# A Perceiver layer on one core: order of the opening, of late loads, and of norm steps

## The chip, the cores and the metric

The kernel runs on one core of a Trainium2 chip. The core has a matrix engine (TensorE, "PE" in the profile, with its weight loads as "PEld"), three engines for elementwise work (VectorE "DVE", ScalarE "ACT", GpSimd "POOL") and an engine that here only issues transfers (SyncE, "SP", its queue "SPq"). Each engine takes its instructions in order and waits on semaphores for the others. The metric is the device time of one execution in microseconds; less is better.

## The reference

Three sub-layers are applied to x, 16 batches of 64 rows of 512 (1024 rows in all), each with a residual: a cross-attention in which the layer-normed x supplies the latents, a differential self-attention over the 64 rows of a batch, and a gated feed-forward whose inputs and weights are rounded to blockwise FP4.

```
x = x + xattn(ctx, layernorm(x))
    ln = LN(latents) * g_l + b_l;  xn = LN(ctx) * g_x + b_x
    q = ln @ w_q;   k, v = split([xn ; ln] @ w_kv)
    out = LN(softmax(q k^T / 8, over 512 context rows and the 64 latents) v @ w_out) * g_o + b_o
x = x + attn(layernorm(x))
    rope on q and k; o = softmax(q1 k1) v - lam * softmax(q2 k2) v; rms norm; @ Wo^T
x = x + ffn(layernorm(x))
    h = silu(fp4(x) @ fp4(w_gate)^T) * (fp4(x) @ fp4(w_up)^T);  fp4(h) @ fp4(w_down)^T
```

All inputs are float32.

## The kernel before

The 1024 rows of x are eight tiles of 128 rows (`cm.x[0]` to `cm.x[7]`), two batches to a tile. The precision of float32 is kept by splitting both factors of a product into a high half, rounded to the matrix engine's float32r, and a low half, the remainder. A product is then three terms, high x high, high x low and low x high, each over four slices of 128 of the inner dimension: `Common.terms` (L114) issues one term per step of a generator, `Common.product` runs all three. Making the halves is a cast (mostly ScalarE) and a subtraction (VectorE or GpSimd).

The program has four stages:

- `_latents` (L455) normalises the tiles of x, turns each on PE (`turn`), scales and shifts it while it is copied out of PSUM (`ln`, L518 and L520), makes its halves (`halves`, L523) and multiplies by w_k, w_q and w_v, two tiles (a "group") at a time. `heads` (L589) makes k or q of a group: four products `lk_g_m` or `lq_g_m` of 128 x 256, each copied to `kst` or `qst` by `take`; `values` makes v. The results go to DRAM. For the first group's k, the variable `late` makes the products of m = 0, 1 and 2 issue their first two terms one product after the other, and the third terms only afterwards, since the low halves of w_k come last. Side work (the weights of w_v, the scaled weights for the context, the bias sums, the statistics of later tiles, the first context batches) is put on a list with `during(n, ...)`; `then()`, called once after each product, runs what the list has for that number.
- `cross_attention` (L723) takes one batch b after another: keys and values of the 512 context rows (`pk`, `pv`), scores (`sim`), a masked softmax, the weighting (`av`). `begin(b)` loads the mask, the queries and the latents' values of a batch, `around(b, m)` loads the latents' keys into the two ends of a key tile. `cx.load(b)` loads the whole context of a batch (`nat`, 1 MB) for its statistics, `cx.fetch` the transposed context in four pieces. `load_o` and `weight_o` load and split w_out during batch 0. Once the first batch is under way, `quant.tick()` runs a step of the FP4 rounding of the feed-forward weights.
- `SelfAttention.rest` (L1362) runs the tiles of the self-attention as a pipeline; the first two are worked in at the end of the cross-attention. In iteration n it makes q, k and v of tile n, adds the output of tile n-2 to x (`out`, the addition at L1339), and `end(n)` makes the transposes, the scores and the softmax. Between these it runs steps of the feed-forward's norm of tiles 0 and 1: `norm_steps` gives seven for a tile, namely moments, shift and scale, and five of the FP4 rounding. `parts[n]` says how many steps stand at each of two places of iteration n: after `rope(n, "Wk")` and after `out(n - 2)`.
- `FeedForward.rest` runs gate, up and down products for the eight tiles.

What sets the order: up to the end of `SelfAttention.rest` the instructions of an engine run in the order in which the program lists them (`Common.in_order`, called at its end, ties each one to the one before it on its engine). Only the rest of the feed-forward is placed by the scheduler of the framework, which may put its instructions among earlier ones. SP's transfers, too, are issued in program order, and a transfer whose buffer is still in use, or whose completion semaphore is still taken by an earlier one, holds up all transfers behind it.

PSUM has three buffers for products and transposes (`cm.mm`, `cm.tr`), two double ones for scores (`cm.two`), and one more. Weights on their way to be split have nine buffers (`raw`): eight are taken by w_k and w_q and the ninth by the first quarter of w_v; the other three quarters of w_v wait until halves of w_k are done.

The opening's order before, as `_latents` lists it: load x tile 0, the four vectors of the norm (`cw.load`), x tile 1, w_k, w_q, the first of w_v, x tiles 2 and 3; moments of both tiles; norm of both; turn of both; halves (high, then low) of tile 0; the casts of w_k; halves of tile 1; the low halves of w_k, those of k = 1 and 3 on GpSimd; then w_q likewise.

Of the kernel before, what the change touches and what calls it, by code (L numbers as in the profile page):

```python
# [14 lines left out]
ALU = mybir.AluOpType  # L15
# [4 lines left out]
P = 128  # L20
# [25 lines left out]
def f32(t):  # L46

    return t.bitcast(F32)
# [406 lines left out]
def _latents(ctx, tc, cm, sc, i, cw, cx, sa):  # L455
# [22 lines left out]
    def high(name, w, k):  # L478
        nc.scalar.copy(w[0][:, k, :], raws[name, k])

    def low(name, w, k):
        by = (nc.vector, nc.gpsimd)[k % 2]
        by.tensor_tensor(w[1][:, k, :], raws[name, k], f32(w[0][:, k, :]), ALU.subtract)

    def split(name, w, *ks):
# [34 lines left out]
                nc.scalar.activation(ln[:, k, :], src, AF.Identity, bias=bias, scale=scale)  # L520
        rows[p] = ln

    def halves(p):  # L523
        g, n = divmod(p, GT)
        ln = rows.pop(p)
        hi, lo = (t[:, :, n * P : (n + 1) * P] for t in lns[g])
        nc.vector.tensor_copy(hi, ln)
        nc.vector.tensor_tensor(lo, ln, f32(hi), ALU.subtract)

    def bias(name, k):  # L530

# [45 lines left out]
    def during(n, do, *args):  # L577

        todo.setdefault(n, []).append((do, args))
# [9 lines left out]
    def heads(g, what, w, dst, scale, bias=None):  # L589

        hi, lo = lns[g]
        st = pool.tile([P, KC, GT * P], F32, tag=f"{what}st", name=f"{what}st_{g}")

        def take(m, ps):
            if bias is None:
                nc.scalar.copy(st[:, m, :], ps)
            else:
                nc.scalar.activation(
                    st[:, m, :], ps, AF.Identity, bias=bias[:, m : m + 1], scale=scale
                )  # L600


        late = 3 if (g, what) == (0, "k") else 0
        made = []
        for m in range(KC):
            cols = slice(m * P, (m + 1) * P)
            ps = cm.mm(f"l{what}_{g}_{m}")[:, : GT * P]
            terms = cm.terms(
                ps,
                lambda k, cols=cols: (w[0][:, k, cols], w[1][:, k, cols], hi[:, k, :], lo[:, k, :]),  # L610
                range(KC),
            )
            made.append((m, ps, terms))
            if m < late:
                next(terms)
                next(terms)
            if m < late - 1:
                continue
            for at, done, steps in made:
                for _ in steps:  # L620
                    pass
                then()
                take(at, done)
            made = []
        nc.sync.dma_start(dst[g], st)

    def values(g):
# [11 lines left out]
            nc.scalar.copy(vst, ps)  # L639
            nc.sync.dma_start(sc.v[p], vst)  # L640

    load(0)
    cw.load(pool)
    load(1)
    weight("k", *range(KC))
    weight("q", *range(KC))
    weight("v", 0)
    load(2, 3)
    moments(0)
    moments(1)  # L650
    cw.turn()
    norm(0)
    norm(1)
    high("k", w_k, 0)
    turn(0)
    turn(1)
    halves(0)
    for k in range(1, KC):
        high("k", w_k, k)
    halves(1)  # L660
    for k in range(KC):
        low("k", w_k, k)
    for k in range(KC):
        high("q", w_q, k)
    for k in range(KC):
# [4 lines left out]
    cx.load(0)  # L670
    for k in range(KC):
        during(0, bias, "q", k)
    during(3, bias_sum, "q", cw.bq, S**-0.5)
    during(16, sa.turn_norm)
    for k in range(KC):
        during(1 + k, high, "v", w_v, k)
# [31 lines left out]
    during(19, cx.load, 1)  # L708
    during(22, cx.every, 0)
    during(39, cx.spread, 1)  # L710
    during(39, cx.load, 2)
    for g, _ in enumerate(groups):
        heads(g, "k", w_k, sc.k, 1.0)
        heads(g, "q", w_q, sc.q, S**-0.5, cw.bq)
        if g + 1 < len(groups):
            for p in groups[g + 1]:
                turn(p)
                halves(p)
        values(g)
    assert not todo  # L720

# [1 line left out]
def cross_attention(tc, cm, sc, i, cw, cx, w1, w2, att, quant):  # L723
# [259 lines left out]
    mask(0)  # L983
    around(0, 0, 1, 2, 3)
    around(1, 0, 1)
    for b in range(B):

        def tick():
            if b:
                quant.tick()  # L990

        done = (b - 3) // 2 if b >= 3 and b % 2 else None
        last = b == B - 1
        keys(b, 0)
        if last:
            att.load("Wq")
            att.load("Wk")
        cx.high(b + 1, 0)
        if b >= 4 and b % 2 == 0:
            out_moments((b - 4) // 2)  # L1000
        tick()
        keys(b, 1)
        cx.low(b + 1, 0)
        cx.high(b + 1, 1)
        tick()
        if b:
            turn_both(b - 1)
            turn_latents(b - 1)
        if done is not None:
            out_turn(done)  # L1010
        keys(b, 2)
        cx.fetch(b + 2, 0)
        cx.flat(b + 1)
        cx.low(b + 1, 1)
        cx.high(b + 1, 2)
        tick()
        if last:
            att.split("Wq", 0, 1)
        if b:
            finish(b - 1)  # L1020
        tick()
        if last:
            att.split("Wq", 2)
        scores(b, 0)
        softmax(b, 0)
        around(b + 1, 2, 3)
        keys(b, 3)
        cx.fetch(b + 2, 1)
        cx.low(b + 1, 2)
        cx.high(b + 1, 3)  # L1030
        tick()
        values(b, 0)
        cx.every(b + 1)
        cx.low(b + 1, 3)
        cx.stats(b + 2, 0)
        tick()
        if last:
            att.split("Wq", 3)
            att.load("Wv")
        if b == 0:  # L1040
            load_o(0)
            load_o(1)
        values(b, 1)
        begin(b + 1)
        cx.fetch(b + 2, 2)
        cx.stats(b + 2, 1)
        tick()
        if b == 0:
            weight_o(0)
            weight_o(1)  # L1050
            load_o(2)
            load_o(3)
        if last:
            att.norm(0)
            att.split("Wk", 0, 1)
        turn(b, 0, 0)
        turn(b, 0, 1)
        scores(b, 1)
        softmax(b, 1)
        around(b + 2, 0, 1)  # L1060
        if done is not None:
            out_product(done)
        quant.tick()
        values(b, 2)
        cx.fetch(b + 2, 3)
        cx.stats(b + 2, 2)
        quant.tick()
        if done is not None:
            out_norm(done)
            out_add(done)  # L1070
        if b == 0:
            weight_o(2)
            weight_o(3)
        if b == 2:
            att.sa.load()
        if b == 5:
            att.sa.work()
        if last:
            att.split("Wk", 2, 3)
            att.load("Wo")  # L1080
            att.turn(0)
        values(b, 3)
        cx.stats(b + 2, 3)
        cx.spread(b + 2)
        mask(b + 1)
        quant.tick()
        cx.load(b + 3)
    turn_both(B - 1)
    turn_latents(B - 1)
    att.product(0, "Wq")  # L1090
    att.split("Wv", 0, 1)
    finish(B - 1)
    att.rope(0, "Wq")
    att.split("Wv", 2, 3)
    att.norm(1)
    att.product(0, "Wk")
    att.rope(0, "Wk")
# [14 lines left out]
    att.norm(2)  # L1112
    out_product(NT - 1)
    att.split("Wo", 2, 3)
    att.end(1)
    out_norm(NT - 1)
    assert not quant.active and not quant.jobs
    return {2: lambda: out_add(NT - 1), 3: lambda: out_moments(NT - 1)}

# [1 line left out]
class SelfAttention:  # L1121
# [240 lines left out]
    def rest(self, ff, last):  # L1362
# [2 lines left out]


        first, second = (ff.norm_steps(t) for t in range(2))
        norms = iter(first[:5] + second[:1] + first[5:] + second[1:])


        parts = {3: (1, 1), 4: (1, 1), 5: (2, 2), 6: (2, 1), 7: (1, 2)}

        def steps(n, part):
            for _ in range(parts[n][part] if n in parts else 0):
# [2 lines left out]
        for n in range(2, NT):  # L1377
# [21 lines left out]
                ff.weights(("g", 0), ("u", 0))  # L1399
            steps(n, 1)  # L1400
            self.end(n)
        assert not list(norms)
        ff.gate((0, 0))
        self.scale(NT - 2)
# [292 lines left out]
```

## Time and profile before

The median of three runs is 925.25 us (924.92 to 925.33). The profile is of one execution, which took 924.27 us; its span, from the first to the last instruction, is 922.5 us. One line of a timeline has the start in us, the busy time in us, engine, line of the code, operation, output and inputs by their names, shapes and count; in brackets stands how long the engine had been idle and what ended it.

| stretch, us | what runs | PE idle in it, us |
|---|---|---|
| 0 to 20 | loads, first norms, first k products | 12.6 |
| 20 to 92 | the rest of the latents' stage | 0.0 |
| 92 to 135 | batch 0 and the start of batch 1 of the cross-attention | 3.0 |
| 135 to 574 | batches 1 to 15 | 0.0 |
| 574 to 725 | self-attention | 5.0 |
| 725 to 922.5 | feed-forward | 4.5 |

The matmuls of the first products (128 x 256) follow each other every 0.213 us until 19.0 us and every 0.12 us from then on. In the middle of the kernel a product of 128 x 512 (12 matmuls) takes PE 2.7 us, one of 128 x 256 1.44 us.

### The profile page before, as it was taken

The page shows a single profiled execution, that of the slowest core. Times are in us where ns is not written, and L with a number is a line of the kernel's source. Part 1 is how long each engine was busy: PE and PEld are TensorE (multiplying, and loading weights), DVE is VectorE, ACT ScalarE, POOL GpSimd, SP SyncE. Part 2 cuts the span into 40 slices and gives each one's busy share as a digit, 9 for nine tenths or more (in the row PEclk, how much of TensorE's full clock was granted, in tenths as well). Part 3 has the DMA queues.
Part 4 walks back from the last instruction along what each step waited for, and adds up shares of the span by engine and source line. Part 5 has one row for each costly group of instructions (what it writes and reads, how often), then busy time and mean ns, then how long its engine had stood idle before and what let it go on. Part 6 is the DMA issues. An engine that isn't in the chain of part 4 may idle for free.

```text
span 922.5 us, 17526 instructions
## 1 busy us (share of the span) xinstructions
PE 897.4 (97%) x6774; PEld 741.2 (80%) x6774; DVE 683.2 (74%) x1384; ACT 392.3 (43%) x750; POOL 328.4 (36%) x378
## 2 busy tenths in 40 slices
PE   4999999999999999999999999999999999999998
PEld 4998778778877887887878877777888788888886
DVE  6545457878799787786987864575888698888875
ACT  4465255544545444444444445444344333323221
POOL 3245143326344363263443622556474321100000
PEclk9999999999999999999999999999999999999999
DMA  6464556454555455345544351140005630000000
GB/s 232 180 222 145 161 149 189 137 182 145 162 142 162 152 163 170 111 141 146 168 137 150 122 177 70 47 183 1 2 1 201 234 137 12 12 12 12 12 12 23
DMA packets 80234, 111.11 MB, mean 120 GB/s; under 512 B 33160, under 2 KB 38808, under 8 KB 78872
## 3 DMA queue, kind: packets, MB, share of 16 engines
q1 hardware_dynamic: 79992, 109.48, 36.9%
q8 instruction: 53, 0.87, 0.4%
q0 software_dynamic: 160, 0.52, 0.2%
q14 instruction: 29, 0.24, 0.1%
HBM read 84.26 MB, written 25.72 MB: 119 GB/s over the span
## 4 chain that ended last, share of the span: by engine, by line
PE 84%; DVE 7%; ACT 3%; POOL 2%; DMA 2%; SPq 1%; issue 1%; ACTq 0%; DVEq 0%; POOLq 0%
PE pv L121 18%; PE pk L121 18%; PE gu L121 13%; PE dn L121 7%; PE av L898 4%; PE sim L830 4%; PE prt L171 3%; PE lk L121 3%; PE lq L121 3%; PE lv L121 2%; PE po L121 2%; PE wo L121 2%; DVE ex L1239 1%; PE Wv L121 1%; PE ht L171 1%
## 5 line engine op out<-in xcount | busy, mean ns | idle before, releaser
L121 PE MATMUL pv<-xvh,x 128*128 128x512 f32 x512 | 133.4, 392 | 1.1 <-ACT prT L865 1.1
L121 PE MATMUL pk<-x,xkh 128*128 128x512 f32 x512 | 130.4, 397 | 0.0
L121 PEld LDWEIGHTS pv<-xvh,x 128*128 128x128 f32 x512 | 95.2, 188 | 24.7 <-issue 2.6
L121 PEld LDWEIGHTS pk<-x,xkh 128*128 128x128 f32 x512 | 93.7, 188 | 25.4 <-issue 3.9
L817 ACT ACTIVATE v<-pv,rs 128x512 f32<-128x512 f32 x64 | 43.9, 686 | 78.8 <-PE pv L121 78.7
L804 DVE TENSOR_TENSOR k<-pk,row 128x512 f32<-128x512 f32 x64 | 43.7, 684 | 45.1 <-PE pk L121 45.1
L368 POOL TENSOR_TENSOR x<-raw,x 128x512 fp32r<-128x512 f32 x32 | 44.2, 1383 | 79.4 <-ACT x L362 79.4
L853 ACT ACTIVATE pr<-pr,least 128x576 f32<-128x576 f32 x64 | 49.2, 772 | 52.4 <-DVE least L849 52.1
L121 PE MATMUL pk<-x,xkl 128*128 128x512 f32 x256 | 68.6, 390 | 0.0
L121 PE MATMUL pv<-xvl,x 128*128 128x512 f32 x256 | 68.5, 389 | 0.0
L121 PE MATMUL gu<-uT,fx 128*128 128x512 f32 (+1 forms) x288 | 67.2, 377 | 0.0
L121 PE MATMUL gu<-gT,fx 128*128 128x512 f32 (+1 forms) x288 | 65.5, 375 | 1.1 <-DVE h L1533 0.6
L121 PEld LDWEIGHTS gu<-gT,fx 128*128 128x128 f32 x288 | 52.3, 188 | 9.0 <-ACT fx L129 0.9
L121 PEld LDWEIGHTS gu<-uT,fx 128*128 128x128 f32 x288 | 51.9, 188 | 7.3
L121 PEld LDWEIGHTS pk<-x,xkl 128*128 128x128 f32 x256 | 48.1, 188 | 10.3
L121 PEld LDWEIGHTS pv<-xvl,x 128*128 128x128 f32 x256 | 48.1, 188 | 10.2
L849 DVE CUSTOM_DVE_ANT_0 pr<-sim,mask 128x576 f32<-128x576 f32 x64 | 45.9, 755 | 9.9 <-PE sim L830 9.1
L121 PE MATMUL dn<-dT,hh 128*128 128x512 f32 x176 | 44.8, 394 | 0.6 <-ACT hh L129 0.6
L205 ACT ACTIVATE qe_h<-qe_h,mmagic 128x512 f32<-128x512 f32 (+1 forms) x24 | 16.5, 688 | 67.2 <-DVE qe_h L202 64.0
L321 DVE BATCH_NORM_STATS2 cst<-nat 128x6 f32<-128x512 f32 x64 | 42.8, 669 | 0.0
L865 ACT COPY prT<-prt 128x512 f32<-128x512 f32 x64 | 34.1, 585 | 18.0 <-PE prt L171 18.0
L898 PEld LDWEIGHTS av<-v,prT 128*64 128x64 f32 x1024 | 36.7, 138 | 5.6 <-issue 5.6
(303 smaller groups left out, 1972.7 us busy)
## 6 DMA issues: line engine op xcount, KB each, us to landing
nat<-in_ctx_dram SPq DMA_DIRECT2D x16, 1024.0 KB
raw<-in_ctxT_dram SPq DMA_DIRECT2D x64, 256.0 KB
d_d<-qhl_d SPq DMA_DIRECT2D x11, 512.0 KB
row<-rs_d SPq DMA_DIRECT2D x16, 256.0 KB
g_d<-qhl_g SPq DMA_DIRECT2D x8, 512.0 KB
u_d<-qhl_u SPq DMA_DIRECT2D x8, 512.0 KB
gT<-g_d SPq DMA_DIRECT2D x4, 1024.0 KB
uT<-u_d SPq DMA_DIRECT2D x4, 1024.0 KB
```

The source lines that it names most:

```text
L121: self.nc.tensor.matmul(ps, lhsT=p[i], rhs=p[j], start=start and n == 0, stop=stop and n == last)
L171: self.nc.tensor.transpose(pt[:, c * P : (c + 1) * P], src[:, c * P : (c + 1) * P], self.ident)
L205: nc.scalar.activation(e, e, AF.Relu, bias=self.mmagic, scale=MAGIC)
L321: nc.vector.bn_stats(st, self.nat[b][:, j, :])
L368: by.tensor_tensor(lo, self.raw[:, c, :], f32(hi), ALU.subtract)
L804: nc.vector.tensor_tensor(k[:, S : S + N], ps, cx.row[b], ALU.mult)
L817: nc.scalar.mul(v, ps, cx.rs[b][:, t : t + 1])
L830: nc.tensor.matmul(pss[r][c * S : (c + 1) * S, h, :half], lhsT=queries[b % 2][rows, m, :], rhs=st["k"][m][rows, at : at + half], start=Tru ...
L849: nc.vector.tensor_tensor_reduce(two(pr), ps[:, :, :half], two(mask), -1.0, BIG, ALU.add, ALU.min, least)
L853: nc.scalar.activation(pr, pr, AF.Exp, bias=least, scale=-1.0, accum_out=st["tot"][:, t : t + 1])
L865: nc.scalar.copy(prT, pt.rearrange("p (j q) -> p j q", q=P))
L898: nc.tensor.matmul(st["av"][rows, 2 * a + r, :], lhsT=w[:, rows], rhs=v[:, at : at + S], start=(n == 0), stop=(n == len(pairs) - 1),)
```

## The change

- The loads of x tiles 0 and 1 are issued first, ahead of the norm's vectors. norm(0) stands ahead of moments(1) on VectorE.
- `halves` is cut in two: `upper` makes the high half of a tile, `lower` the low one. Both tiles' high halves come first, then both low ones. All four low halves of the first w_k are made by VectorE; the others keep their alternation between VectorE and GpSimd.
- In `heads`, the products that are made together (three for the first k, one elsewhere) issue their first terms, then their second, then their third. Their calls of `then()` all come next, and only then the copies. For the first q the copies lag two products behind (`lag`), and the bias sum of q moves from list number 3 (with k's last product) to 5 (with q's second).
- `cx.load(2)` moves from the end of the latents' stage behind the first `around` loads of the cross-attention.
- w_out: `weight_o(0)`, `weight_o(1)` and the loads of quarters 2 and 3 move, within batch 0, from after `values(0, 1)` to after `values(0, 2)`; `weight_o(2)` and `weight_o(3)` move to batch 1, after `keys(1, 1)`.
- At the end of the cross-attention, quarters 2 and 3 of Wv are split ahead of `finish(B - 1)`, and `out_norm(NT - 1)` stands ahead of `att.end(1)`.
- The norm steps have a third place, after `end(n)`; the order of the two tiles' steps and their shares change. First-tile steps are f0 to f6 and second-tile steps s0 to s6: before, n = 3: f0 | f1; 4: f2 | f3; 5: f4 s0 | f5 f6; 6: s1 s2 | s3; 7: s4 | s5 s6. After, n = 3: f0 | - | f1; 4: f2 s0 | f3 | s1; 5: f4 | f5 | f6; 6: s2 | s3 | -; 7: s4 | s5 | s6.

```diff
-    def low(name, w, k):
-        by = (nc.vector, nc.gpsimd)[k % 2]
+    def low(name, w, k, by=None):
+        by = by or (nc.vector, nc.gpsimd)[k % 2]
...
-    def halves(p):
-        g, n = divmod(p, GT)
-        ln = rows.pop(p)
-        hi, lo = (t[:, :, n * P : (n + 1) * P] for t in lns[g])
-        nc.vector.tensor_copy(hi, ln)
-        nc.vector.tensor_tensor(lo, ln, f32(hi), ALU.subtract)
+    def upper(*tiles):
+        for p in tiles:
+            g, n = divmod(p, GT)
+            nc.vector.tensor_copy(lns[g][0][:, :, n * P : (n + 1) * P], rows[p])
+
+    def lower(*tiles):
+        for p in tiles:
+            g, n = divmod(p, GT)
+            hi, lo = (t[:, :, n * P : (n + 1) * P] for t in lns[g])
+            nc.vector.tensor_tensor(lo, rows.pop(p), f32(hi), ALU.subtract)
...
         late = 3 if (g, what) == (0, "k") else 0
-        made = []
+        lag = 2 if (g, what) == (0, "q") else 0
+        made, ready = [], []
...
             made.append((m, ps, terms))
-            if m < late:
-                next(terms)
-                next(terms)
             if m < late - 1:
                 continue
-            for at, done, steps in made:
-                for _ in steps:
-                    pass
+            for _ in range(3):
+                for _, _, steps in made:
+                    next(steps)
+            for _ in made:
                 then()
-                take(at, done)
+            ready += made
             made = []
+            while len(ready) > lag:
+                take(*ready.pop(0)[:2])
+        for at, done, _ in ready:
+            take(at, done)
...
-    load(0)
+    load(0, 1)
     cw.load(pool)
-    load(1)
...
     moments(0)
-    moments(1)
     cw.turn()
     norm(0)
+    moments(1)
     norm(1)
     high("k", w_k, 0)
     turn(0)
     turn(1)
-    halves(0)
     for k in range(1, KC):
         high("k", w_k, k)
-    halves(1)
+    upper(0, 1)
+    lower(0, 1)
     for k in range(KC):
-        low("k", w_k, k)
+        low("k", w_k, k, nc.vector)
...
-    during(3, bias_sum, "q", cw.bq, S**-0.5)
+    during(5, bias_sum, "q", cw.bq, S**-0.5)
...
-    during(39, cx.load, 2)
...
                 turn(p)
-                halves(p)
+                upper(p)
+                lower(p)
...
     around(1, 0, 1)
+    cx.load(2)
...
         keys(b, 1)
+        if b == 1:
+            weight_o(2)
+            weight_o(3)
...
-        if b == 0:
-            weight_o(0)
-            weight_o(1)
-            load_o(2)
-            load_o(3)
...
         if b == 0:
-            weight_o(2)
-            weight_o(3)
+            weight_o(0)
+            weight_o(1)
+            load_o(2)
+            load_o(3)
...
     att.split("Wv", 0, 1)
+    att.split("Wv", 2, 3)
     finish(B - 1)
     att.rope(0, "Wq")
-    att.split("Wv", 2, 3)
...
     att.split("Wo", 2, 3)
+    out_norm(NT - 1)
     att.end(1)
-    out_norm(NT - 1)
...
-        norms = iter(first[:5] + second[:1] + first[5:] + second[1:])
-        parts = {3: (1, 1), 4: (1, 1), 5: (2, 2), 6: (2, 1), 7: (1, 2)}
+        norms = iter(first[:3] + second[:1] + first[3:4] + second[1:2] + first[4:] + second[2:])
+        parts = {3: (1, 0, 1), 4: (2, 1, 1), 5: (1, 1, 1), 6: (1, 1, 0), 7: (1, 1, 1)}
...
             self.end(n)
+            steps(n, 2)
```

## The prediction

> **What bounds the kernel.** The page's first part shows PE busy 97% of 922.5 us, so only places where PE waits can pay. The table of stretches (length, PE busy with its instructions, clock, DMA share, GB/s) says where these are:
>
> ```profile
> 0.00:20.00 20.00, 7.39 (x33) 1.00 0.66 223
> 20.00:92.00 72.00, 72.00 (x505) 1.00 0.52 186
> 92.00:135.00 43.00, 40.05 (x279) 1.00 0.57 166
> 135.00:574.00 439.00, 439.00 (x3336) 1.00 0.49 149
> 574.00:725.00 151.00, 145.98 (x1654) 1.00 0.24 93
> ```
>
> Between 20 and 92 us and between 135 and 574 us PE never rests: a PE instruction that comes earlier there brings the end forward one for one. The losses are 12.6 us in the opening, 3.0 where the cross-attention starts, 5.0 in the self-attention; the change touches all three. The waits of PE, and the timeline around them:
>
> ```profile
> PE lk L121 <- DVE lnh L527: 5.7, 1, 5.7
> PE pv L121 <- ACT prT L865: 1.1, 1, 1.1
> PE av L898 <- ACT prl L883: 1.0, 1, 1.0
> PE sim L830 <- DMA mask<-q_d: 0.9, 1, 0.9
> ```
> ```profile
> 9.94 2.67 POOL L483 TENSOR_TENSOR wkl<-raw_k,wkh 128x512 fp32r<-128x512 f32 x2 [2.51 <-ACT wkh L479]
> 10.41 1.08 DVE L527 CAST lnh<-ln 128x512 fp32r<-128x512 f32 x1
> 11.52 1.64 DVE L528 TENSOR_TENSOR lnl<-ln,lnh 128x512 fp32r<-128x512 f32 x1
> ...
> 13.08 1.48 DVE L527 CAST lnh<-ln 128x512 fp32r<-128x512 f32 x1
> 14.60 1.64 DVE L528 TENSOR_TENSOR lnl<-ln,lnh 128x512 fp32r<-128x512 f32 x1
> ...
> 14.71 1.20 PE L121 MATMUL lk<-lnh,wkh 128*128 128x256 f32 x4 [5.70 <-DVE lnh L527]
> ```
>
> The first product waits for the second tile's first half, which ends at 14.56, behind the first tile's second half. Each of these four VectorE steps takes over twice its undisturbed time (0.43 and 0.69 us at 31.81 and 32.27), while GpSimd makes weight halves.
>
> **Opening (loads, halves, staged terms).** SP issues x tile 1 at about 1.18 instead of 2.57; the four vector rows move back 0.4 us and land at about 4.5, wanted by ScalarE's ln at 7. On VectorE norm(0) now comes before moments(1): GpSimd's mv is ready at 5.24, so norm(0) runs at 5.3 (was 6.06), moments(1) at 5.8, its GpSimd pair until 7.7, norm(1) 7.7 to 8.25 (was 7.84: 0.4 later). PE turns tile 1 by 9.4, VectorE's four ln steps (1.37) end at 10.9. Then both casts: 0.43 each, GpSimd idle, since its k halves are gone and its q halves wait for raw_q 1, which ScalarE casts until 12.28. So hi is complete at 11.8 and PE starts at 11.85, 2.85 earlier. The twelve first terms need only that; at the cold pitch of 0.213 they last until 14.4.
>
> Here a rule must be weighed. By the rows, a VectorE step beside GpSimd is slower by 1.64/0.69 = 2.4; so counted, the second lo ends at 14.0, the k halves at 15.3, 15.9, 16.5 and 17.1. The Trainium skill (SBUF — State Buffer, "Who interferes with whom") says instead that a VectorE instruction with two SBUF inputs, or in a two-port mode, and a GpSimd one lock each other out for a whole instruction. That fits the ends better: GpSimd's four subtractions (9.94 to 15.69) and VectorE's four halves end in strict turn, at 11.20, 11.49, 12.61, 13.16, 14.28, 14.56, 15.69, 16.24. I take it. GpSimd keeps q halves 1 and 3: the first holds up lo 1 (ends 14.05), the second k half 0 (ends 15.75); the others follow at 16.4, 17.0, 17.6. Second terms: 14.4 to about 16.8. Third terms of m=0 wait for k half 3: done 17.8; m=1 and m=2 (0.48 each) 18.8.
>
> Product m=3 needs the PSUM buffer of m=0, hence its copy on ScalarE, and all three `then()` now precede it: it queues behind the casts of v 0 and v 1. raw_v 1 takes the buffer of a weight half; the first one went at 11.20 (GpSimd's half 1), now at 15.75. SP issues it at 15.8, it lands about 2.7 later (its row: 11.23 to 13.75 and on), cast until 19.2, copy until 19.6. So m=3 starts at 19.65, ends at 21.1. The bias sum (0.9) moves from before q to after q's second product, so q ends at 21.1 + 4x1.44 + 0.9 = 27.8, against 29.57. **Gain 1.8** (by the factor 2.4 it would be 2.35). If that raw load is late there is less: 0.8; with no wait for it 2.6. The q copies, two products late, wait for bq at about 25.0, before q's last product wants the buffer. norm(3) then ends at about 27.4, just in time: VectorE is next in line.
>
> A second rule speaks against hoping for more: the Trainium skill (TensorE: Matmul & The Clock Gate, Part 1) has the first 3.4 us or so of activity at half clock whatever is issued, by a free-running window. The row: cold pitch 0.213 from 14.71 to 19.02 (4.3 us), then 0.117. By the row the second terms end at 16.8, by the rule at 15.9, with a missed window at 17.0; each time k half 3 (17.6) and the copy (19.6) decide. Nothing is added for it.
>
> **Cross-attention start.** nat_2 (1 MB, SP at 90.62) now goes after the `around` loads.
>
> ```profile
> 93.85 0.64 SPq L762 DMA_DIRECT2D mask<-q_d  x1
> ...
> 98.84 0.45 SPq L792 DMA_DIRECT2D k<-k_d  x1
> 99.59 0.44 SPq L793 DMA_DIRECT2D k<-k_d  x1
> ...
> 100.80 2.23 PE L830 MATMUL sim<-k,mask 64*64 64x288 f32 x16 [0.88 <-DMA mask<-q_d]
> 101.50 0.19 PEld L830 LDWEIGHTS sim<-k,mask 64*64 64x64 f32 x2 [0.51 <-DMA k<-k_d]
> 101.85 0.67 PEld L830 LDWEIGHTS sim<-k,mask 64*64 64x64 f32 x10 [0.16 <-DMA k<-k_d]
> ```
>
> The 128 KB of queries took 6.8 us to land beside it, and SP's k issue at 98.84 waited 1.36 on nat's completion semaphore. Without it that pair goes at 97.5 and 98.15, lands 2.25 later (as 99.59 to 101.85) at 100.4, and PE resumes there instead of at 101.85: **gain 1.45** (0.7 to 2.0). nat_2 is then issued at about 104.4 (in the old run's times). Its first reader stands on VectorE at 107.56 and may wait to about 110; next in that queue is the softmax minimum at 113.5, with statistics of 1.8 between: room, cost 0.
>
> weight_o(0, 1) leaves ScalarE's queue ahead of prT: there the casts at 115.55 waited 3.35 for raw_wo, and PE lost 1.24 at 117.45. Now prT copies run at about 112, **gain 1.2**. SP also loses the two load_o that held the k loads and the first qw_g behind them, so VectorE no longer waits for qw_g (8 us idle before 124.53). The bill comes in batch 1: weight_o(2, 3), 1.24 of ScalarE and 2.6 of GpSimd, now stand ahead of prT and prl for which PE lost 1.17 at 131.26; VectorE's exponent mask (1.52 beside GpSimd at 127.69) is still ahead of them too. Ends: all 1.17 gone, or 0.6 more. I take **0.5 gained**.
>
> **Self-attention.** Wv's halves 2 and 3 before finish(15): GpSimd's last one moves from 590.50 to 584.9, PE's 0.5 at 591.85 goes: **0.5**; VectorE and GpSimd are idle there, and rc_k follows in time. out_norm before end(1): oz (0.81 at 617.33) moves to about 609.4, into an idle of 2.45 on VectorE; the `on` that PE awaits starts 0.7 earlier, still after GpSimd's rstd at 617.1: **0.7** of the 0.93 at 618.79. Norm steps: at n=3 the ScalarE step fz (642.75, waiting 2.86 for mv_f) moves behind end(3), so qT comes 1.0 earlier and PE's wait at 644.09 goes: **1.0**. But at n=4 begin of tile 1 joins slot 0, ahead of the x addition that frees wt's buffer:
>
> ```profile
> 657.60 1.22 DVE L196 TENSOR_SCALAR qm_x<-qs_x 128x32 f32<-128x32 f32 x1
> 658.85 0.35 DVE L197 RECIPROCAL qm_x<-qm_x 128x32 f32<-128x32 f32 x1
> 659.12 0.63 DVE L1339 TENSOR_TENSOR x<-wo,x 128x512 f32<-128x512 f32 x1
> ```
>
> The addition is already late by 0.3; bn_stats and bn_aggr (0.69 + 0.18 + a gap) add **1.0 lost** (0.7 to 1.3). At n=6 the step fz leaves but qm's four remain behind GpSimd's adds: 0. n=5 and n=7 have cover (the addition ran as soon as wo ended): 0.
>
> **Sum.** 1.8 + 1.45 + 1.2 + 0.5 + 0.5 + 0.7 + 1.0 - 1.0 = 6.15. The profiled execution took 924.27 (span 922.5 and 1.8 around it) and becomes 918.1; the median, 925.25, is 1.0 above it and becomes **919.1**.
>
> **Rivals.** (a) As worked out, each term within its ends: 917.5 to 920.5, 0.60. (b) The opening hardly pays: raw_v 1, or norm(3), holds PE until 29; the opening gives 0.3, total 4.6, 920.6; for it: all raw loads are bandwidth-bound here (223 GB/s), against: SP issues nothing else at 15.8. 0.14. (c) ScalarE's wo casts move PE's loss to batch 1 (131.26 grows by 0.6) and the k loads still land late: total about 4.0, 921.3. 0.12. (d) The n=4 loss doesn't come, since the scheduler's order leaves VectorE free earlier: 917.5 or below, 0.09. (e) Slower: nat_2 lands late. VectorE stands in order at its statistics, and behind it the softmax minimum of batch 0's second half; PE wants what follows (pr turned at 126) 11 us after it. Landing 8 us after issue (as at 90.62) costs nothing; from 17 us on each us is lost, and 24 us would pass 925.25: 926 or more. No transfer of the trace is near that. 0.03. That the parts cancel or the change does nothing: 0.02.
>
> 0.2% (1.85 us) is what a measurement can tell from no change. Faster 0.94, same 0.03, slower 0.03. Range: 916.8 to 921.8, which takes in (b) and (c).
>
> **What would show it.** First lk matmul at about 11.9 and lq's last before 28; no wait at the former 117.45 and 591.85; sim's wait under 0.7; wt at n=4 waiting about 1.5 for x. Wrong if m=3 of lk waits past 20.5, if the av wait doubles, or if VectorE is seen standing at nat_2's statistics beyond 5 us.

## The result, and the profile after

The changed kernel takes 918.08 us (median of four runs, 917.56 to 919.49) against 925.29 for the kernel before in four runs beside it: ratio 0.9925, 95% interval 0.9911 to 0.9939. The profiled execution took 917.56 us, its span is 915.8, so 6.71 of execution and 6.7 of span are gone. Line numbers below are those of the changed kernel, up to 8 off for the same line.

The table of stretches of the kernel after (length, PE busy with its instructions, granted clock, DMA share, GB/s):

```profile
0.00:20.00 20.00, 10.78 (x61) 1.00 0.76 252
20.00:90.00 70.00, 69.17 (x479) 1.00 0.53 183
90.00:130.00 40.00, 39.40 (x283) 1.00 0.59 178
...
570.00:720.00 150.00, 145.56 (x1653) 1.00 0.25 98
```

The opening's loss fell from 12.6 to 9.2 us, that at the cross-attention's start from 3.0 to 0.6, that of the self-attention from 5.0 to 4.4. New is 0.8 us of loss in the stretch from 20 on, which had none before. The waits of PE (line waited for: total, times, longest; the first of the list, for the norm's vectors, is left out) name it:

```profile
PE lt L171 <- DVE lz L155: 3.0, 4, 1.2
PE lk L121 <- DVE lnh L526: 2.3, 1, 2.3
PE wt L1282 <- DVE x L1346: 1.4, 2, 1.1
PE ot L171 <- DVE on L1318: 0.8, 1, 0.8
...
PE av L904 <- ACT prl L889: 0.6, 1, 0.6
```

The wait of lk went from 5.7 to 2.3; those of `pv` for prT and of `sim` for the queries are off the list. Two waits grew: `lt`, the turn of a tile that norm(3) feeds, and `wt`, as forecast.

Where the gain arose is read by lining up the same matmul in both traces. This ledger is worked out from their start times; a negative lead means that the kernel after is ahead.

| at the matmul of (time before) | lead, us | step | forecast |
|---|---|---|---|
| lv, first (30.36) | -2.08 | -2.08 | -1.8 |
| sim of batch 0, last (102.63) | -4.07 | -1.99 | -1.45 |
| pv after prT (117.45) | -5.31 | -1.24 | -1.2 |
| av after prl (131.26) | -5.85 | -0.54 | -0.5 |
| Wv (591.85) | -6.38 | -0.53 | -0.5 |
| ot after `on` (618.79) | -7.31 | -0.93 | -0.7 |
| zt at n = 3 (644.09) | -8.25 | -0.94 | -1.0 |
| wt at n = 4 (659.80) | -7.52 | +0.73 | +1.0 |
| ot at n = 6 (685.71) | -6.81 | +0.71 | 0 |
| end | -6.69 | +0.12 | |

Every term came with its sign and within about half a us, but for the last +0.71, which was not foreseen. The step at `av` is the least certain: the experiments show how far it varies.

The opening's inside went otherwise than worked out. The timeline of the kernel after, VectorE and GpSimd from 10 us on (start, busy):

```profile
10.81 0.76 DVE L526 CAST lnh<-ln 128x512 fp32r<-128x512 f32 x2
11.48 1.29 DVE L532 TENSOR_TENSOR lnl<-ln,lnh 128x512 fp32r<-128x512 f32 x2
12.68 2.50 DVE L483 TENSOR_TENSOR wkl<-raw_k,wkh 128x512 fp32r<-128x512 f32 x4
15.09 1.29 DVE L483 TENSOR_TENSOR wql<-raw_q,wqh 128x512 fp32r<-128x512 f32 x2
11.36 7.61 POOL L483 TENSOR_TENSOR wql<-raw_q,wqh 128x512 fp32r<-128x512 f32 x2 [3.69 <-ACT wqh L479]
```

The two engines did not take turns. VectorE ran eight two-input steps back to back, one every 0.602 us, and GpSimd's first q half, issued at 11.36, took 6.17 us: it came through after the last of them. So the last k half ended at 15.2, not 17.6; SP could issue raw_v 1 at 13.45, not 15.8; m = 3 of lk started at 18.19 without a wait, not at 19.65; and q ended at 26.4, not 27.8. Then 1.2 us of that lead went at the turns of tiles 2 and 3. The timeline of the kernel after around them:

```profile
24.91 1.29 POOL L483 TENSOR_TENSOR wvl<-raw_v,wvh 128x512 fp32r<-128x512 f32 x1
24.98 1.50 DVE L155 TENSOR_SCALAR lz<-x,mv_l 128x512 f32<-128x512 f32 x1
26.61 0.55 POOL L500 TENSOR_TENSOR mv_l<-mv_l,mhalf 128x1 f32<-128x1 f32 x1
27.20 0.55 DVE L155 TENSOR_SCALAR lz<-x,mv_l 128x512 f32<-128x512 f32 x1 [0.72 <-POOL mv_l L500]
27.89 0.63 PE L171 MATMUL lt<-ident,lz 128*128 128x128 f32 x4 [0.64 <-DVE lz L155]
```

GpSimd's half of w_v's last quarter holds up norm(2) (1.50 instead of 0.55) and its own pair of steps for norm(3), which end at 27.16. norm(3) runs at 27.20, and PE, done with q at 26.4, has to wait for it.

In the cross-attention's start the kernel after does what was forecast (timeline, PE, SP and VectorE):

```profile
97.76 1.20 PE L836 MATMUL sim<-k,mask 64*64 64x288 f32 x16
101.63 0.53 SPq L314 DMA_DIRECT2D nat<-in_ctx_dram  x1
107.42 0.69 DVE L321 BATCH_NORM_STATS2 cst<-nat 128x6 f32<-128x512 f32 x1 [3.42 <-DMA nat<-in_ctx_dram]
109.41 0.76 DVE L855 CUSTOM_DVE_ANT_0 pr<-sim,mask 128x576 f32<-128x576 f32 x1 [0.28 <-PE sim L836]
```

The sixteen `sim` matmuls run in 1.20 us without a wait (2.23 before, after a wait of 0.88). nat_2 landed 5.8 us after its issue; VectorE stood 3.42 us at its statistics, and had 0.28 us left before PE had the scores for the softmax minimum behind them: no cost here. How late nat_2 could land before PE waits for it was not tried.

### The profile page after: what moved, and what is told of

It is laid out like the page before. It is cut to its first block, busy times and chain, and to the rows that moved or that the text cites. A ratio compares the mean times of both kernels' runs of the same rounds, so it can differ in the third digit from the quotient of the medians.

```text
span 915.8 us, 17531 instructions
## 1 busy us (share of the span) xinstructions
PE 896.2 (98%) x6774; PEld 741.3 (81%) x6774; DVE 687.8 (75%) x1386; ACT 392.7 (43%) x750; POOL 330.0 (36%) x376
## 4 chain that ended last, share of the span: by engine, by line
PE 86%; DVE 6%; DMA 2%; ACT 2%; POOL 1%; SPq 1%; issue 1%; ACTq 0%; DVEq 0%; POOLq 0%
PE pk L121 19%; PE pv L121 18%; PE gu L121 13%; PE dn L121 7%; PE av L904 4%; PE sim L836 4%; PE prt L171 3%; PE lv L121 2%; PE po L121 2%; PE lq L121 2%; PE lk L121 2%; PE wo L121 2%; PE Wv L121 2%; PE ht L171 1%; DMA raw_wo<-in_w_out_dram 1%; PE Wq L121 1%
```

## The experiments

All ran with the kernel before beside them (its medians 924.94 to 925.32). The time of a run is given with its ratio to the kernel before; "ledger" is the matmul lead against the kernel after, as above, where plus is later.

| run | us | ratio, 95% interval |
|---|---|---|
| after | 918.08 | 0.9925 [0.9911, 0.9939] |
| opening undone | 920.47 | 0.9942 [0.9927, 0.9957] |
| nat_2 early | 919.64 | 0.9935 [0.9920, 0.9949] |
| w_out early | 923.12 | 0.9977 [0.9966, 0.9989] |
| both early | 921.77 | 0.9965 [0.9952, 0.9978] |
| norm steps as before | 917.31 | 0.9909 [0.9894, 0.9924] |
| norm steps in a third order | 916.35 | 0.9907 [0.9892, 0.9922] |
| k halves shared | 918.22 | 0.9927 [0.9912, 0.9942] |
| moments early | 917.61 | 0.9923 [0.9906, 0.9939] |
| last v half on VectorE | 917.16 | 0.9914 [0.9899, 0.9929] |
| the same, k halves shared | 918.83 | 0.9931 [0.9916, 0.9946] |
| w_out later in batch 1 | 917.25 | 0.9917 [0.9902, 0.9931] |
| three together | 914.65 | 0.9888 [0.9871, 0.9904] |

The kernel after was not run again beside the later runs, and only the intervals of w_out early, both early and three together stand clear of its own. For the other runs the reading rests on the ledger, which compares one execution with one. Its steps vary most at the first `av` of batch 1 (125 us), by up to 0.8 us between runs without an edit near it, and by up to 0.6 from there to 560 us. The traces show what varies at `av`. ScalarE's copies prT and prl stand behind the casts of w_out's second half and behind a step that waits for VectorE's exponent mask (L202). In the kernel after the two casts ran back to back from 121.71 and the mask took 0.42 us. In the run with the third order of norm steps the casts waited for their loads until 121.98 and 122.75 (ledger +0.49), and with the moments early the mask took 1.52 us beside GpSimd (+0.46).

Some parts of the change were never undone alone: the order of the first loads, the staged terms, the lag of the copies and the bias sum in the opening, and the two moves at the end of the cross-attention (Wv's halves and `out_norm`). The steps of -0.53 and -0.93 of those two are read from the ledger only.

### The opening undone

Everything in `_latents` as before, nat_2 kept late:

```diff
-    load(0, 1)
+    load(0)
     cw.load(pool)
+    load(1)
...
-    upper(0, 1)
-    lower(0, 1)
+    halves(1)
     for k in range(KC):
-        low("k", w_k, k, nc.vector)
+        low("k", w_k, k)
```

> The changed kernel with the opening as it was before (loads, halves, staged terms, bias sum and lag). Theory: PE's order after the opening is unbroken up to 90 us, so the 2.1 us that the first v product comes earlier in the changed kernel (28.28 against 30.36) are lost one for one at the end: 920.2, span 917.9. Rival: the transfers and waits at the cross-attention's start take up what the opening gives, so less than 1 us is lost: under 919.1.

920.47. The ledger has +1.96 at the first v product and still +1.9 at 116 us, then +0.8 more up to `av` of batch 1, and +2.8 at the end. So what the opening gives, 2.0, is handed on undiminished, as the first theory had it. The 0.8 arises far from the edit, at the place that varies; the medians differ by 2.4.

### nat_2 back in the latents' stage

```diff
     during(39, cx.spread, 1)
+    during(39, cx.load, 2)
...
     around(1, 0, 1)
-    cx.load(2)
```

> The changed kernel with only the load of nat_2 put back at the end of the latents' stage. Theory: the queries and the first latent keys land late again and the first scores lose 2.0 us (PE's lead over the kernel before grew from 2.1 to 4.1 us there): 920.1. Rival: the lead came from the mask's shorter issue (0.93 to 0.42 us) and the shifted time of the stores, not from nat_2: then under 0.5 us is lost, 918.6 or less.

919.64, 1.6 above the kernel after; the ledger shows +1.9 over the `sim` matmuls, and PE waits 0.86 for the queries again. The move is worth 1.9 where it acts and 1.6 by the medians, where I had 1.45. (The trace ends at +2.7; the other 0.8 comes at `av` and later, without an edit there.)

### w_out at its old places

```diff
-        if b == 1:
-            weight_o(2)
-            weight_o(3)
...
+        if b == 0:
+            weight_o(0)
+            weight_o(1)
+            load_o(2)
+            load_o(3)
...
-            weight_o(0)
-            weight_o(1)
-            load_o(2)
-            load_o(3)
+            weight_o(2)
+            weight_o(3)
```

> The changed kernel with weight_o and load_o where they were before. Theory: ScalarE waits for raw_wo ahead of the prT copies again; PE loses 1.2 us at the fourth pv product of batch 0 and 0.5 at the first av: 919.8. Rival: with nat_2 later, raw_wo lands earlier or ScalarE gets to it later, and nothing is lost: 918.1.

A miss: 923.12, so 5.0 lost where 1.7 was expected. The timeline of this run (SP, ScalarE, PE):

```profile
109.31 0.89 SPq L972 DMA_DIRECT2D raw_wo<-in_w_out_dram  x2
113.69 1.35 ACT L129 CAST woh<-raw_wo 128x512 fp32r<-128x512 f32 x2 [5.67 <-DMA raw_wo<-in_w_out_dram]
114.95 1.07 ACT L871 COPY prT<-prt 128x512 f32<-128x512 f32 x2
115.58 1.69 PE L121 MATMUL pv<-xvh,x 128*128 128x512 f32 x4 [3.39 <-ACT prT L871]
```

The quarters of w_out land 4.4 us after their issue; ScalarE stands in order at their casts, and the prT copies that free PE's buffers stand behind. PE was ready at 112.2 and waited 3.39 us. The ledger has +3.44 there and then +5.16 ten matmuls later, with no further wait. The table of stretches of this run tells why (after the count: granted clock, then DMA share and GB/s):

```profile
110.00:114.00 4.00, 2.19 (x10) 1.00 0.81 279
114.00:118.00 4.00, 2.42 (x7) 0.76 0.72 177
118.00:122.00 4.00, 4.00 (x16) 0.81 0.54 143
```

From 116.2 to 119.2 us the 128x512 matmuls follow each other every 0.427 us instead of 0.227, at half the clock: with the changes of pitch at both ends 1.72 us. So a wait of 3.4 us on PE cost 5.2 at this place. 0.8 of it comes back at the first `av` of batch 1, where the kernel after waits 0.6 for prl and this run doesn't, and 4.4 is left at the end of this trace. The median's 5.0 has more of the clock in it: granted clocks of 0.76 and 0.81 over 4 us each are 3.4 us at half speed, which lowers the mean over 920 us by 0.002. This execution, the fastest of the seven, has a mean of 0.998; the others go down to 0.995, so by this estimate they have one to three such stretches. The four of the kernel after have 0.999 or 1.0.

After this run I took it that nat_2, now ahead of the quarters in SP's queue, makes them late, so that the two moves need each other. The next run asks for that.

### Both loads early

The edits of the last two runs together.

> The kernel after with both late loads undone: nat_2 back in the latents' stage, weight_o and load_o at their old places. Theory (weight_o at its old place is that dear only because nat_2 is now ahead of its raw quarters in SP's queue; the two moves need each other): less is lost than with weight_o alone undone, about 3.2 us as the prediction's terms 1.45 + 1.2 + 0.5 have it, so 921.3. Rival (two separate gains): the sum of the single runs, 1.6 + 5.0, so 924.7.

921.77, near the first number and far from the sum. But the mechanism that I had named is not what the trace shows: with nat_2 long landed the quarters still take 4.5 us (issued 109.53, first cast 114.07), as against 4.4 with it. What differs is PE: held up at `sim` (+2.1), it comes to the prT copies at 116.0, and the wait there is 0.28. The quarters' landing is a date that hardly moves; a PE that is earlier waits longer for it. The moves are in series on one path: the first is worth nothing while the second stands, and with w_out at its old places the median was even higher with nat_2 late (923.12) than with it early (921.77), by the lost clock. This run's profiled execution, too, has a stretch at half the clock, a pitch of 0.427 from 101.6 to 104.2 us, after a wait of 1.12 at `sim`: 1.6 of its 4.9 us at the end. The other four runs of this kernel have a mean clock of 0.999 or 1.0 (0.998 here) and are shorter, so the median, 3.7 above the kernel after, stands for the waits.

### Norm steps as before

```diff
-        norms = iter(first[:3] + second[:1] + first[3:4] + second[1:2] + first[4:] + second[2:])
+        norms = iter(first[:5] + second[:1] + first[5:] + second[1:])
...
-        parts = {3: (1, 0, 1), 4: (2, 1, 1), 5: (1, 1, 1), 6: (1, 1, 0), 7: (1, 1, 1)}
+        parts = {3: (1, 1, 0), 4: (1, 1, 0), 5: (2, 2, 0), 6: (2, 1, 0), 7: (1, 2, 0)}
```

> The changed kernel with the norm steps at the two old places and in the old order. Theory: PE gets back the wait at zt in n=3 (0.94 lost), but not the 0.73 more at wt in n=4 nor the 0.71 at ot in n=6, which the new order brought: 0.5 us faster, 917.6. Rival: the two new waits have other causes (the earlier out_norm, the shifted time), and undoing the steps loses the 0.94 without a return: 919.0.

917.31; the times overlap those of the kernel after, the ledger decides: its steps are +0.9 at zt (n = 3), -0.74 at wt (n = 4) and -0.72 at ot (n = 6), and -0.4 is left at the end. So the new steps as a whole gain nothing; two of the three places take back what the first gives. The third one is this, in the timeline of the kernel after:

```profile
677.17 1.06 POOL L210 TENSOR_TENSOR fz<-fz,qs_x 128x512 f32<-128x512 f32 x1
677.32 0.94 DVE L1263 TENSOR_SCALAR sm<-sm,neglam 128x8 f32<-128x8 f32 x1
678.17 0.68 DVE L1318 TENSOR_TENSOR on<-o,rstd_o 128x512 f32<-128x512 f32 x1
678.91 0.66 PE L171 MATMUL ot<-ident,on 128*128 128x128 f32 x4 [0.79 <-DVE on L1318]
```

Step f6, moved behind end(5), is a multiplication on GpSimd. A tiny VectorE step of 128 x 8 comes 0.15 us after it and takes 0.94 us instead of 0.23; `on`, which PE awaits, stands behind it.

### Norm steps in a third order

The third place kept for n = 3, where it pays; tile 1's first step behind the addition at n = 4, f6 ahead of end(5):

```diff
-        norms = iter(first[:3] + second[:1] + first[3:4] + second[1:2] + first[4:] + second[2:])
+        norms = iter(first[:4] + second[:1] + first[4:] + second[1:])
...
-        parts = {3: (1, 0, 1), 4: (2, 1, 1), 5: (1, 1, 1), 6: (1, 1, 0), 7: (1, 1, 1)}
+        parts = {3: (1, 0, 1), 4: (1, 2, 0), 5: (1, 2, 1), 6: (1, 1, 0), 7: (1, 1, 1)}
```

> The changed kernel with the third place kept for f1 only at n=3, but no step of tile 1 in front of the x addition of n=4 and no GpSimd multiplication behind end(5): n=3: f0, none, f1; n=4: f2, then f3 s0; n=5: f4, f5 f6, s1; n=6 s2, s3; n=7: s4, s5, s6. Theory: the added 0.73 at wt (n=4) and 0.71 at ot (n=6) go, the zt gain of 0.94 stays: 916.6. Rival: s0's statistics or f6 cost the same at their new places: 918.1.

916.35. The timeline of the kernel after at the first of the two places, and below it that of this run at both:

```profile
650.80 0.64 DVE L145 BATCH_NORM_STATS2 st_f<-x 128x6 f32<-128x512 f32 x1
651.47 0.18 DVE L146 BATCH_NORM_AGGREGATE mv_f<-st_f 128x2 f32<-128x6 f32 x1
651.57 0.66 DVE L1346 TENSOR_TENSOR x<-wo,x 128x512 f32<-128x512 f32 x1
652.28 1.15 PE L1282 MATMUL wt<-ident,w 64*64 64x64 f32 x32 [1.11 <-DVE x L1346]
```

```profile
651.37 0.63 DVE L1346 TENSOR_TENSOR x<-wo,x 128x512 f32<-128x512 f32 x1
652.05 1.15 PE L1282 MATMUL wt<-ident,w 64*64 64x64 f32 x32 [0.31 <-DVE x L1346]
...
677.08 0.23 DVE L1263 TENSOR_SCALAR sm<-sm,neglam 128x8 f32<-128x8 f32 x1
677.22 0.68 DVE L1318 TENSOR_TENSOR on<-o,rstd_o 128x512 f32<-128x512 f32 x1
```

The wait of wt is 0.31 (1.11 in the kernel after) and the small step takes 0.23 again. The ledger steps by -0.8 and -0.7 at these places, as much as the new order had lost there: both losses were the order of the steps, and the gain at n = 3 stays.

### The first low halves of w_k shared again

```diff
-        low("k", w_k, k, nc.vector)
+        low("k", w_k, k)
```

> The changed kernel, but low halves 1 and 3 of the first w_k go to GpSimd again. It asks who gets in when VectorE and GpSimd want the same port. Theory (the prediction's, strict turns): GpSimd's k halves run from 9.2 to 11.7, the first cast waits for the second of them and the second cast for GpSimd's q half behind it, so the first lk product starts at 13.4 instead of 11.7 and the end comes about 1.2 later, 919.3. Rival (a waiting GpSimd step gets in only when VectorE has nothing queued, as the changed kernel's two q halves look, 7.6 us for both): both casts follow each other after 11.7, first lk at 12.4, end 918.4.

The time is the rival's (918.22), the start of lk the theory's (13.49). In the timeline of this run the turns are back:

```profile
10.68 2.66 DVE L526 CAST lnh<-ln 128x512 fp32r<-128x512 f32 x2
13.26 2.36 DVE L532 TENSOR_TENSOR lnl<-ln,lnh 128x512 fp32r<-128x512 f32 x2
9.16 2.49 POOL L483 TENSOR_TENSOR wkl<-raw_k,wkh 128x512 fp32r<-128x512 f32 x2 [1.63 <-ACT wkh L479]
11.61 2.86 POOL L483 TENSOR_TENSOR wql<-raw_q,wqh 128x512 fp32r<-128x512 f32 x2
15.54 2.37 DVE L483 TENSOR_TENSOR wkl<-raw_k,wkh 128x512 fp32r<-128x512 f32 x2
15.59 1.78 POOL L483 TENSOR_TENSOR wvl<-raw_v,wvh 128x512 fp32r<-128x512 f32 x1 [1.12 <-ACT wvh L479]
13.49 2.90 PE L121 MATMUL lk<-lnh,wkh 128*128 128x256 f32 x12 [4.20 <-DVE lnh L526]
```

GpSimd had the port first, at 9.16, and both casts of VectorE took 2.66 instead of 0.76. The two rows from 15.5 on show more: there VectorE came first, by 0.05 us, and GpSimd's half of w_v did not have to wait for a row of steps. It got in behind one k half, and the next one took 1.77 us. So being first does not by itself explain the eight steps in a row of the kernel after. But of lk's delay of 1.78 us only 0.91 is left at the turn of tile 2 and 0.08 at that of tile 3: the wait for norm(3) hides it. (Later places of this trace add 0.3 at `av` and 0.2 in the later batches; both differ by as much between runs without an edit near them, so I don't put these down to the edit. The medians differ by 0.1.) The next three runs ask whether norm(3) is what hides it.

### Moments of tiles 2 and 3 one number earlier

```diff
-        during(2 + k, low, "v", w_v, k)
+        during(2 + k + k // 3, low, "v", w_v, k)
...
-        during(first + n % 2, moments, n)
-        during(first + 2, norm, n)
+        during(first + (n % 2 if n > 3 else 0), moments, n)
+        during(first + (2 if n > 3 else 1), norm, n)
```

> The changed kernel with the moments of x tiles 2 and 3 both on list number 4 and their norms on number 5, and the low half of w_v 3 (GpSimd) on number 6, behind them. Theory: the transposes of tiles 2 and 3 lose 1.2 us in the changed kernel since GpSimd's w_v half stands before tile 3's rstd and locks out tile 2's norm; this goes: 916.9. Rival: w_v's half then comes late for the first v product's second term and gives it back: 918.1.

A miss: 917.61, and the ledger gains only 0.40 at the turn of tile 3, gone by the end. norm(3), at 25.84, still took 1.51 us beside GpSimd's v half, one number later as well, and bq came later with the moments ahead of it, for which q's last product waited 0.36. What had to go was the neighbour, not the place.

### The last low half of w_v on VectorE

```diff
-        during(2 + k, low, "v", w_v, k)
+        during(7 if k == 3 else 2 + k, low, "v", w_v, k, nc.vector if k == 3 else None)
```

> The kernel after, but the low half of the last quarter of w_v is made by VectorE, two list numbers later, so that no GpSimd subtraction stands ahead of norm(3). Theory (norm(3), locked out behind that subtraction, is what holds tile 3's transposes): the second wait of lt, about 0.8 to 1.2 us, goes: about 917.0. Rival (the transposes would then wait for something else at nearly the same time, as in the run with the early moments, which gained 0.4 there): 917.7 or no difference.

917.16. The timeline of this run:

```profile
24.96 0.55 DVE L155 TENSOR_SCALAR lz<-x,mv_l 128x512 f32<-128x512 f32 x1
25.96 0.55 DVE L155 TENSOR_SCALAR lz<-x,mv_l 128x512 f32<-128x512 f32 x1 [0.45 <-POOL mv_l L500]
26.16 1.11 PE L171 MATMUL lt<-ident,lz 128*128 128x128 f32 x8
```

Both norms take 0.55, and the eight turns run through without a wait: ledger -1.24 there. 0.57 of it goes at `av` of batch 1, and -0.5 reaches the end in the trace; the medians differ by 0.9. What holds prl there in this run is not w_out's casts, which end at 121.53, but the exponent mask: it took 1.52 us beside GpSimd, and prT follows only at 123.36.

### The same, with w_k's halves shared

> The kernel of the run before this one (w_v's last low half on VectorE) with the first w_k's low halves 1 and 3 on GpSimd again. With norm(3) in the way these cost only 0.1. Theory (norm(3) hid the cost of sharing, 0.9 at the transposes of tile 2): now it shows, about 0.9 above the run before this one, 917.9. Rival (the sharing doesn't matter, since q's halves are made in turn anyway): within 0.2 of it.

918.83, 1.7 above the run before it; in the traces lk starts 1.82 later, q's end is 1.5 later, and 1.3 is left at the end. With norm(3) out of the way the sharing that had cost 0.1 (0.6 in the trace) costs 1.7 (1.3 in the trace), more than I expected (0.9). In the trace 1.4 is there at the first v product and 0.8 behind `av`; 0.35 of the 1.3 at the end comes in the self-attention, far from the edit, and the four executions spread over 1.4 us, so the size is rough. So VectorE making all of w_k's low halves pays only when the next bound is lifted too.

### w_out's second half behind turn_latents in batch 1

```diff
         keys(b, 1)
-        if b == 1:
-            weight_o(2)
-            weight_o(3)
...
             turn_latents(b - 1)
+        if b == 1:
+            weight_o(2)
+            weight_o(3)
```

> The changed kernel with weight_o(2, 3) behind turn_latents of batch 1 instead of before. Theory: prT and prl no longer queue behind the two casts (1.27 with a wait for raw_wo), the 0.6 to 0.8 at av goes: 917.4. Rival: the exponent of the first weight rounding (ScalarE waits for VectorE) is what holds prl, as before the change: 918.1.

917.25; ledger -0.63 at `av`. This is what weight_o(2, 3) ahead of prT and prl still cost in the kernel after.

### Three together

The last v half on VectorE, the third order of the norm steps, and the last edit.

> The kernel after with three edits together: w_v's last low half on VectorE, the norm steps in the order of the earlier run (f2 f3 and then s0; f4, f5 f6, s1), and weight_o(2), weight_o(3) behind turn_latents in batch 1. Theory (three separate places of the path): 918.1 - 1.1 - 1.7 - 0.8 = 914.5. Rival (some are covered by a wait that comes later): above 915.5.

914.65, 3.4 below the kernel after and ratio 0.9888 to the kernel before. The ledger has -1.13 at the turns, -1.95 at `av`, -2.52 at wt, -3.23 at ot and at the end. The waits of PE in this run:

```profile
PE wt L1282 <- DVE x L1346: 0.6, 2, 0.3
...
PE av L904 <- ACT prl L889: 0.2, 1, 0.2
```

The waits are each taken away where they arise, so they add up here: the single runs lie 0.92, 1.73 and 0.83 below the kernel after, 3.48 together.

## Why the prediction was right, point by point

**The total**: 6.15 forecast from the profiled execution, 6.71 measured there, 7.21 by the medians. The first case held, and 918.08 is inside its own range; each term that was given ends came within them. That the total is so near is in part luck: by the ledger the terms came out better than forecast by 1.4 in sum and worse by 0.9, 0.7 of it at a place that had been put at nothing.

**The opening, 1.8 forecast, 2.1 measured: the size held, two steps in it did not.** PE's start (11.85 forecast, 11.71 measured) was right: the high halves first, with GpSimd idle, take 0.76. Wrong was "strict turn" for the steps from 11.4 on: that row came from a stretch in which GpSimd was at work first. With VectorE there first, GpSimd waited for 6.17 us (though not in every such case, as the run with w_k's halves shared shows). This made the k halves 2.4 us earlier and raw_v 1's issue too, so the forecast bound (the copy behind v 1's cast, 19.65) never bound. Wrong, too, was "norm(3) then ends at about 27.4, just in time: VectorE is next in line". It ended at 27.75, behind GpSimd's half of w_v, and became the bound. The runs with the last v half on VectorE (-1.24 at the turns) and with w_k's halves shared in both settings (0.1, then 1.7) show it. The two errors had opposite signs, so that the size came out right by luck. Without the second the opening gives 3.3 (lead of the run with the last v half on VectorE at the first v product), more than the forecast's alternative of 2.6 with no wait for raw_v.

By the Trainium skill (SBUF — State Buffer, "Who interferes with whom") the engine that issues first has the shared port for the whole instruction and the other blocks fully. The rows agree as to blocking: 6.17 for a step of GpSimd's, 0.94 for VectorE's 128 x 8. They differ from what I had added to it, that the port changes hands after each instruction. It did in the kernel before and with w_k shared (casts of 1.25 and 1.48 us). It did not during VectorE's eight steps in the kernel after.

**The clock**: the row's pitch of 0.213 held until 16.4, the second terms ended at 16.75 (16.8 by the row, 15.9 by the rule). That nothing was to be added was right. Worked again as estimates from the same start and figures, the two come out at 16.6 and 16.2, nearer to each other than I had them. And the hit says little: with the same first products the pitch changed anywhere from 14.6 to 17.4 us in the traces of the other runs.

**nat_2, 1.45 forecast, 1.99 measured**, at the upper of its ends: the wait for the queries ahead of the first `sim` matmul went (0.96 of the step is there at that matmul), and so did the stalls between the sixteen (1.03). The cost, 0, was right.

**w_out, 1.2 and 0.5 forecast, 1.24 and 0.54 measured.** The first is right as a term of this sum, in this order. Missing was that it is worth far more once nat_2 is out of the way: without it the kernel after loses 5.2 at that place, 3.4 of wait and 1.7 of clock. The second was taken between two ends 1.8 us apart, and `av` varies by up to 0.8 between traces: that it came to 0.54 is luck.

**Self-attention**: 0.5, 0.7 and 1.0 forecast as gains, 0.53, 0.93 and 0.94 measured; 1.0 as loss at n = 4, 0.73 measured. The step that failed is "n=5 and n=7 have cover ...: 0". I looked for the wait of the addition's reader and for each moved step's own engine, and not at who would stand beside f6's GpSimd multiplication once it ran behind end(5): 0.71 lost, and 0.72 regained by the run with the old steps.

**The rivals**: the second one named norm(3) as what might hold PE until 29. It did hold it, until 27.89, but from a better start. The third (w_out's bill in batch 1) was real as a rest of 0.63 at `av`, not as a growth. The fourth, no loss at n = 4, fell. The slower one, nat_2 late, didn't come: 5.8 us to land, where by the forecast 17 would have begun to cost.

## What to carry to other kernels

A step that is moved brings its neighbours with it: list, for each place it moves to, what the other engine on the shared port runs there, down to 8-column steps, and what stands behind them. Where a gain disappears at the next bound (0.1 against 1.7 for the same edit), take the next bound away before judging the edit, and judge terms in series one after another rather than by undoing them singly. A load whose cast stands ahead of work that PE needs belongs behind that work.

## What the runs showed of the hardware that was not expected

- Blocking at the shared port can go on past one instruction, or not. In the kernel after and nine other runs with the same opening, eight two-input steps of VectorE ran at 0.602 us each while a GpSimd subtraction took 5.7 to 6.2 us. Where GpSimd had been at work first, the two alternated, and VectorE's casts took 1.25 and 1.48 us instead of 0.42. But in both runs with w_k's halves shared a GpSimd subtraction that came at the same time as a VectorE one, or 0.05 us after it, got in behind that single step. What decides it is open.
- A wait of PE can cost the clock: after 3.39 us of waiting, 128x512 matmuls ran at a pitch of 0.427 us instead of 0.227, 1.72 us lost; in another run the same pitch came after a wait of 1.12 us and stalls of 0.95 us among the matmuls behind it. By the granted clock (0.76 and 0.81 over 4 us each; 0.72 over 6 us) both stretches lasted 3.4 us. In the profiled execution of the kernel before, a wait of 0.88 at the same place had no such consequence; some of its other executions have a mean clock of 0.998, and where they lost it is not known. The Trainium skill (TensorE: Matmul & The Clock Gate, Part 1) has an idle window of some 3.4 us bring the half clock back; that fits the first case, the second came with less.
- The first matmuls' time at half clock is no constant, not even for one opening: with the first lk matmul at 11.6 to 11.8 us the pitch changed 3.0 to 5.7 us later in ten traces (4.7 in the kernel after). That is in keeping with the free-running window of the same page.
